# A four-layer graph network on one Trainium2 core: variances of a layer's late part by ACT, sends held back, ring places freed by the block

## The chip, the cores and the metric

The kernel runs on one core of a Trainium2 chip, in one launch. The engines are TensorE (PE; its weight loads are listed as PEld), VectorE (DVE), ScalarE (ACT), GpSimd (POOL) and SyncE (SP). The metric is the device time of the launch in microseconds (us). The kernel before takes 1677.57 us, the median of eight runs, which lie between 1672.64 and 1680.2.

## The reference

4096 nodes with 256 features each go through four graph attention layers over the same symmetric 0/1 adjacency matrix with about nine neighbours a row, the node itself included. Each layer adds to x what attention makes of a normed x:

```python
h = jnp.maximum(_layernorm(x, axis=-1), 0.0)        # (x - mean) / sqrt(var + 1e-5), then relu
x = x + layer(h, adj, ...)

# layer 0, 4 heads of 64
Wh = (h @ W).reshape(n, heads, d)
e = leaky_relu(s_i[:, None, :] + s_j[None, :, :], 0.2)   # s: Wh times the halves of a
e = where(adj == 0, -inf, e); alpha = softmax(e, axis=1)
out = elu(einsum('ijh,jhd->ihd', alpha, Wh))

# layer 1, one head:  h @ W + softmax(masked leaky_relu(s1 + s2, 0.01)) @ node
# layer 2, four heads: like layer 0 with biases, slope 0.2, no elu
# layer 3, four heads: softmax(q k^T / 8 + mask) v, with q, k, v = h @ Wq + bq, ...
```

The adjacency matrix is an input, so the kernel has to find the neighbours itself.

## The kernel before, in words

The rows are sorted by their number of neighbours and cut into 32 blocks of 128 rows. All rows of a block have the same number of slots (`CAPS[b]`, 23 in block 0 down to 3 in block 31), of which layers 1 to 3 gather at most 15; rows of block 0 with more neighbours share an extra place. A *gather* (`fetch`, L993) is an indirect DMA issued by POOL: 128 rows of a table in DRAM, one for each partition, go to one place of a ring in SBUF (`RING` = 18432 floats a partition; 69 places of 264 floats in the late part of layer 0 and in layer 2, 64 of 288 in layer 1, 36 of 512 in layer 3). A *send* (`send`, L1010) is the opposite: 128 rows go to their places in a table or, in layer 3, in the output. The tables `tab[0]` to `tab[3]` hold what the neighbours of each layer need.

The stages, by the profile:

- 0 to some 362 us: the matrix is read, the neighbour lists are made, the rows are sorted, and the first six slots of layer 0 are worked off on the way.
- `late()`, 364.7 to 542.7: the rest of layer 0, in 19 groups (`LATE`) of one or two blocks, 14 of which still have something to gather (17 places for block 0 in turn 3, then 8, 7 and fewer a block down to 1). It is pipelined by hand: turn i does `scores(i)`, then parts of `settle` for groups i-2, i-1, i-3 and i-2, then `weigh(i)`, then a part of `settle(i-1)`. PE, DVE, ACT and SP run in the order in which the program is written. POOL's order is chained by `turn` dependences: `fill(i)` first sends every finished block (`deliver`), and then issues the gathers of the groups up to i+4.
- `layer(1)` 542.7 to 903.3, `layer(2)` to 1268.2, `layer(3)` to the end: blocks in the order `ORDER`, gathers ahead as far as the ring has room (`fill`), every engine in program order.

In a turn of `late()`, `scores` adds the two halves of the score (L1132), takes the leaky relu (L1136), has ACT copy the row's old maximum beside them (L1137), takes the maximum (L1140), subtracts it (L1141) and has ACT take exp (L1146). `weigh` makes the sum and the shares (L1162 to L1166), multiplies the row's earlier result and the gathered rows with them (L1170, L1184) and sums them on PE (L1178, L1190). `settle` has five parts:

1. ACT makes exp of the sum, minus 1 (L1201, L1202);
2. DVE makes elu plus x (L1204, L1205), and `norms_of` the mean and variance, `bn_stats` and `bn_aggr` a block (L642, L643); ACT then makes 1/sqrt(var + eps) to first order by Ln, Identity, Exp and Square (L648, L652, L653, L655);
3. DVE does a Newton step (L659, L661, L664), ACT norm and relu (L1214), PE the transposes (L1221);
4. ACT copies them (L1224), PE multiplies with layer 1's weights (L986);
5. DVE adds layer 1's own product to x (L1231), ACT writes scores and list beside it (L1232, L1233), and the block is ready to send to `tab[1]`.

`known()` makes what later stages need of the lists (as float numbers, with marks where a slot is empty); it is called in turn 1. It waits on DVE for the lists' reload (L804) and has one iota on POOL (L807).

In `layer(l)`, `weigh` sums in one PSUM tile: x (L1450), the row's own share (made at L1454, product at L1458), then the gathered slots, multiplied by DVE eight at a time (L1466) and two to a matmul (L1471). A gather that reuses a place of the ring waits for all the products that read it, as the tile framework finds them. `settle` sums the two halves of the PSUM tile; in layer 3 that is the result, one of three buffers of two kinds in turn (L1487), which is appended to `made`. After each block `third` sends what is in `made`:

```python
while made and (len(made) > 1 or todo == []):
    self.send(*made.pop(0))
```

so one result is held back as long as there are gathers left (`todo`), and then all go.

Of the kernel before, what the change touches and what calls it, by code (L numbers as in the profile page):

```python
# [19 lines left out]
P = 128  # L20
# [60 lines left out]
class Sparse:  # L81
# [938 lines left out]
    def layers(self):  # L1020
        tc, nc, nt = self.tc, self.nc, self.nt
        with ExitStack() as ctx:
            big = self.big = ctx.enter_context(tc.tile_pool(name="s_big", bufs=1))
            self.pacc = ctx.enter_context(tc.tile_pool(name="s_pacc", bufs=4, space=PSUM))
            shares = ctx.enter_context(tc.tile_pool(name="s_pe", bufs=1, space=PSUM))
            self.pp = ctx.enter_context(tc.tile_pool(name="s_pp", bufs=3, space=PSUM))

            self.turns = 0
            self.shares = shares.tile([P, IB], F32, name="s_shares")

            rx = self.all = big.tile([P, nt, D + WL], F32, name="s_rx")
# [9 lines left out]
            self.has = big.tile([P, nt, CAPS[0]], F32, name="s_has")  # L1041
            E = mybir.EngineType
# [13 lines left out]
    def late(self):  # L1056
# [26 lines left out]
            self.fetched = f  # L1083
            return f

        def deliver():
            while pending:
                b = pending.pop(0)
                s = self.send(self.tab[1], self.own(b), self.listed[b]).ins
                if self.fetched is not None:  # L1090
                    self.turn(s, self.fetched)
                between.append(s)
                self.tc.declare_no_dep(s, group="rows", reason="places differ")
                self.tc.add_to_no_dep_group("rows", s)
                self.told.append(s)

        def fill(i):
            nonlocal at
            deliver()
            while todo and todo[0] <= i + 4:  # L1100
                m, K = size(todo[0])
                s = (at if at + m * K <= slots else 0) if K else 0
                if any(s < e and b < s + m * K for b, e in held.values()):
                    return
                j = todo.pop(0)
                for u, b in enumerate(LATE[j]):
# [88 lines left out]
        def settle(i):  # L1195
# [9 lines left out]
            nc.vector.scalar_tensor_tensor(xt, acc, 0.0, ex, ALU.max, ALU.add)  # L1205
            norm = self.norms_of(pool, xt if m > 1 else xt[:, 0, :], m, f"0_{i}", self.minus)
            for _ in range(m if m > 1 else 0):
                next(norm)
            next(norm)
            yield  # L1210
            rn = next(norm)
            h = part(i, D, 2 * D)
            for u in range(m):
                nc.scalar.activation(  # L1214
                    h[:, u, :], xt[:, u, :], AF.Relu,
                    bias=rn[:, m + u : m + u + 1], scale=rn[:, u : u + 1],
                )
            pt = self.pp.tile([P, IB], F32, tag="ps", name=f"s_pht_0_{i}")
            for u in range(m):
# [24 lines left out]

        for i in range(len(LATE) + 3):
            fill(i)
            if i == 1:
                self.known()
            if i == 5:
                self.share_place()  # L1250
            if i < len(LATE):
                scores(i)
            go_on(i - 2)
            go_on(i - 1)
            go_on(i - 3)
            go_on(i - 2)
            if i < len(LATE):
                weigh(i)
                del held[i]
            go_on(i - 1)  # L1260
        deliver()

    def layer(self, l):
# [5 lines left out]
        ring = self.ring[:, : slots * wide].rearrange("p (k w) -> p k w", w=wide)  # L1269
        todo, held, at = list(ORDER), {}, 0  # L1270
        made = []

        def fill(i):
            nonlocal at
            while todo and nt - len(todo) <= i + AHEAD:
# [11 lines left out]
                if l == 3:  # L1287
                    vs[j] = self.pool.tile([P, D], F32, name=f"s_vself_{j}", tag="vself", bufs=5)
                    nc.sync.dma_start(out=vs[j], in_=self.tab[3][ts(j, P), D:])
                for k in range(K):  # L1290
                    at_k = self.near[:, j, k : k + 1]
                    g = self.fetch(ring[:, s + k, :], self.tab[l], at_k).ins
                    for told in self.told:
                        self.tc.add_manual_dep(
                            g, told.name,
# [32 lines left out]
        def third(d):  # L1328
            if d in rows:
                next(rows.pop(d), None)  # L1330
            while made and (len(made) > 1 or todo == []):
                self.send(*made.pop(0))

        S, N = 1, 2
        for i in range(nt):
# [10 lines left out]
            del held[b]  # L1346
            settle(c)
        z, y, x, w = ORDER[-1:-5:-1]

# [9 lines left out]
    def scores(self, l, b, mine, g):  # L1359
# [8 lines left out]
        if l < 3:  # L1368
# [2 lines left out]
                nc.scalar.activation(e[:, :G, 0], g[:, :G, D], AF.Identity, bias=src)  # L1371
                nc.scalar.activation(e[:, K, :], mine[:, D : D + H], AF.Identity, bias=src)
            else:
                nc.vector.tensor_tensor(e[:, K, :], mine[:, D : D + H], src, ALU.add)
# [11 lines left out]
            nc.vector.scalar_tensor_tensor(ek, ek, slope, ek, ALU.mult, ALU.max)  # L1386
        else:
            q = self.shares[:, IB - D :]
            nc.scalar.copy(q, mine[:, 0:D])
# [31 lines left out]
    def mutual(self, b, g):  # L1421
# [7 lines left out]
        nc.vector.tensor_reduce(self.has[:, b, :K], eq[:, :K, :], AX.X, ALU.max)  # L1429

    def weigh(self, l, b, me, g, made):

# [7 lines left out]
        if tot is None:  # L1440
# [9 lines left out]
        nc.tensor.matmul(  # L1450
            acc[:, 1, :], lhsT=self.ident, rhs=self.x[b], start=True, stop=False
        )
        mev = pool.tile([P, D], F32, name=f"s_me_{l}_{b}", tag="me", bufs=3)
        nc.vector.tensor_tensor(  # L1454
            mev.rearrange("p (h d) -> p h d", h=H), me.rearrange("p (h d) -> p h d", h=H),
            p[:, K, :].unsqueeze(2).to_broadcast([P, H, D // H]), ALU.mult,
        )
        nc.tensor.matmul(acc[:, 0, :], lhsT=self.ident, rhs=mev, start=False, stop=False)  # L1458
        if more:
            rows = self.more_rows(l, p, g[:, KEPT, :])  # L1460
            nc.tensor.matmul(acc[:, 0, :], lhsT=self.to_row, rhs=rows, start=False, stop=False)
        step = 2 if b in ORDER[-2:] else AT_ONCE
        for k0 in range(0, G, step):
            m = min(step, G - k0)
# [1 line left out]
            nc.vector.tensor_tensor(  # L1466
                v, v, p[:, k0 : k0 + m, :].unsqueeze(3).to_broadcast([P, m, H, D // H]), ALU.mult
            )
            for k in range(k0, k0 + m, 2):
                n = min(2, G - k)  # L1470
                nc.tensor.matmul(  # L1471
                    acc[:, 0:n, :], lhsT=self.ident, rhs=g[:, k : k + n, v0 : v0 + D],
                    start=False, stop=(k + 2 >= G),
                )
        return acc

    def settle(self, l, b, acc, made):
# [5 lines left out]
        if l == 3:  # L1483
# [4 lines left out]
            made.append((self.out, self.own(b), y))  # L1488
            yield None
            return  # L1490
        nc.vector.tensor_reduce(xt, acc.rearrange("p u d -> p d u"), AX.X, ALU.add)
        yield from self.normed(pool, xt, f"{l + 1}_{b}")

    def advance(self, l, b, ht, made):
# [35 lines left out]
    def symmetric(self):  # L1530

        nc, ok = self.nc, self.ok[:, 4:5]
        nc.vector.scalar_tensor_tensor(
            self.has, self.away[:, :, : CAPS[0]], 1.0 / FAR, self.has, ALU.mult, ALU.max
        )
        nc.vector.tensor_reduce(self.both[:, 0:1], self.has, AX.XY, ALU.min)
        nc.vector.tensor_reduce(ok, self.both, AX.X, ALU.min)
        nc.vector.tensor_scalar(ok, ok, 0.5, None, ALU.is_ge)
# [564 lines left out]
```

## Time and profile before

| what | value |
|---|---|
| median of 8 runs | 1677.57 us (1672.64 to 1680.2) |
| the profiled execution: its time, its span | 1676.78 us, 1675.1 us |
| mean clock granted to TensorE | 0.817 of full speed |
| busy: PE, DVE, ACT, POOL | 1099.8, 1104.6, 541.5, 1143.8 us |
| gathers from the ring stages on (L993 into `s_ring`) | 900, 952 ns each |
| sends of layer 0's late part, of layer 3 | 32, 32 |

In a line of the profile the first number (or the first two) is a start or a busy time in us; `x900` is a number of instructions; `out<-in` names the tiles; a bracket or a last column tells how long the engine had been idle before, and what ended that. "issue" stands for idle time in which the engine waited for nothing that the profile shows. All times are of one execution.

### The profile page before, as it was taken

The numbers are of one execution on the slowest core, as the hardware profiler recorded it, in microseconds if no ns is written. First come the engines' busy times: TensorE is split into PE (matmuls) and PEld (weight loads), VectorE is DVE, ScalarE is ACT, GpSimd is POOL, SyncE is SP. The second block draws the span as 40 slices with busy tenths as digits, with TensorE's granted clock in tenths as the row PEclk, the third lists the DMA queues.
The fourth block names the chain that finished last, engine by engine and source line by source line (L and its number), as shares of the span: only waits on it lengthen the run. The fifth ranks groups of instructions, "written<-read, shape, count | busy, mean of one in ns | idle before, by whom it ended". The sixth has DMA issues, their size and how long they took to land. (4 is left out here: it accounts for less than half of the span.)

```text
span 1675.1 us, 14506 instructions
## 1 busy us (share of the span) xinstructions
PE 1099.8 (66%) x3035; PEld 572.7 (34%) x3035; DVE 1104.6 (66%) x2651; ACT 541.5 (32%) x1754; POOL 1143.8 (68%) x1241
## 2 busy tenths in 40 slices
PE   5868878705775377777773787878782655556445
PEld 4523333203443144444442344444441322222222
DVE  5669899816885255555552576667674897877776
ACT  6966664003344133333332133333341000000000
POOL 1277777767774777777773777777755777777774
PEclk9969999857898678788786798989996777677777
DMA  7899999466552444444442444444435776767663
GB/s 267 301 395 394 353 394 326 145 218 166 153 167 69 119 128 133 131 132 130 133 131 65 116 132 133 134 132 133 133 109 169 222 212 196 210 191 212 196 188 112
DMA packets 125912, 309.11 MB, mean 185 GB/s; under 512 B 35028, under 2 KB 53463, under 8 KB 125816
## 3 DMA queue, kind: packets, MB, share of 16 engines
q0 software_dynamic: 66832, 203.64, 41.7%
q1 hardware_dynamic: 58984, 104.46, 17.5%
q8 instruction: 28, 0.46, 0.1%
q14 instruction: 68, 0.56, 0.1%
HBM read 273.00 MB, written 35.00 MB: 184 GB/s over the span
## 5 line engine op out<-in xcount | busy, mean ns | idle before, releaser
L993 POOL DMA_INDIRECT s_ring<-s_tab,s_near x900 | 857.0, 952 | 325.9 <-issue 240.5
L1471 PE MATMUL s_acc<-s_ring,s_ident 128*128 128x512 f32 (+1 forms) x858 | 425.9, 647 | 28.9 <-DVE s_ring L1466 28.9
L993 POOL DMA_INDIRECT s_g<-s_tab,s_keep x192 | 182.8, 952 | 130.9 <-DMA s_raw<-in_adj_dram 66.5
L1471 PEld LDWEIGHTS s_acc<-s_ring,s_ident 128*128 128x128 f32 x858 | 185.0, 220 | 249.9 <-issue 181.8
L1466 DVE TENSOR_TENSOR s_ring<-s_ring,s_shares 128x2048 f32<-128x2048 f32 (+1 forms) x153 | 232.8, 1552 | 0.0
L1458 PE MATMUL s_acc<-s_me,s_ident 128*128 128x256 f32 x192 | 77.6, 494 | 130.8 <-DVE s_me L1454 130.8
L277 ACT ACTIVATE s_low<-s_raw 128x1024 fp8e4<-128x1024 int32 x128 | 135.1, 1055 | 65.7 <-DMA s_raw<-in_adj_dram 64.5
L986 PE MATMUL s_ps<-s_we_l,s_ht 128*128 128x264 f32 x256 | 95.8, 520 | 91.8 <-ACT s_ht L976 68.2
L1418 ACT ACTIVATE s_shares<-s_e 128x40 f32<-128x40 f32 (+7 forms) x64 | 13.0, 203 | 344.4 <-DVE s_e L1415 344.3
L986 PE MATMUL s_ps_kv<-s_wkv,s_ht 128*128 128x512 f32 x128 | 80.4, 761 | 63.6 <-ACT s_ht L976 63.6
L1394 DVE TENSOR_TENSOR s_ring<-s_ring,s_shares 128x2048 f32<-128x2048 f32 (+7 forms) x47 | 78.7, 1675 | 65.3 <-DMA s_ring<-s_tab,s_near 45.4
L519 PE MATMUL s_pt<-s_low,s_mark_True 128*128 128x512 fp8e4 x256 | 83.3, 405 | 54.4 <-DVE s_cand L531 48.7
L531 DVE MAX8 s_cand<-s_pt 128x8 f32<-128x256 f32 x256 | 93.1, 416 | 13.8 <-PE s_pt L529 13.8
L1426 DVE TENSOR_SCALAR s_eq<-s_ring,s_own_f 128x207 bf16<-128x207 f32 (+12 forms) x32 | 12.2, 382 | 136.0 <-DMA s_ring<-s_tab,s_near 135.7
L986 PEld LDWEIGHTS s_ps<-s_we_l,s_ht 128*128 128x128 f32 x256 | 57.5, 243 | 118.8 <-ACT s_ht L976 80.7
L629 PE MATMUL s_ae<-s_g,s_ident 128*128 128x512 f32 x192 | 93.9, 619 | 3.5 <-DVE s_g L620 3.5
L956 ACT ACTIVATE s_y<-s_mv,s_eps 128x1 f32<-128x1 f32 x64 | 18.9, 295 | 232.3 <-DVE s_mv L953 125.7
L1458 PEld LDWEIGHTS s_acc<-s_me,s_ident 128*128 128x128 f32 x192 | 43.0, 240 | 148.8 <-DVE s_me L1454 142.9
L1397 DVE TENSOR_REDUCE s_e<-s_ring 128x32 f32<-128x2048 f32 (+7 forms) x47 | 78.9, 1679 | 1.6
L1375 DVE TENSOR_TENSOR s_e<-s_ring,s_rx 128x36 f32<-128x36 f32 (+12 forms) x32 | 6.3, 197 | 103.6 <-DMA s_ring<-s_tab,s_near 81.2
L1450 PE MATMUL s_acc<-s_rx,s_ident 128*128 128x256 f32 x192 | 67.6, 439 | 0.0
L519 PEld LDWEIGHTS <-s_mark_True 128*128 128x128 bf16 x256 | 23.2, 101 | 107.7 <-issue 63.6
(284 smaller groups left out, 1787.6 us busy)
## 6 DMA issues: line engine op xcount, KB each, us to landing
s_raw<-in_adj_dram SPq DMA_DIRECT2D x128, 512.0 KB, 9.7
s_ring<-s_tab,s_near POOLq DMA_INDIRECT x900, 2.9
s_rx<-s_placed SPq DMA_DIRECT2D x32, 262.0 KB, 3.1
s_tab<-s_kv SPq DMA_DIRECT2D x32, 256.0 KB, 2.5
s_tab<-s_rx SPq DMA_DIRECT2D x32, 132.0 KB, 2.0
s_keep<-in_x_dram SPq DMA_DIRECT2D x8, 512.0 KB, 8.9
s_vself<-s_tab SPq DMA_DIRECT2D x32, 128.0 KB, 3.4
s_tab<-s_keep SPq DMA_DIRECT2D x7, 528.0 KB, 3.9
```

The lines of the kernel that those rows point to most:

```text
L277: nc.scalar.activation(low[r][:, quarter(q)], raw.pop(q), AF.Copy, saturate=False, accum_out=self.sums[:, r, h : h + 1],)
L519: nc.tensor.matmul(pt, lhsT=self.mark[k], rhs=lo[:, k * PAIR + g * IB : k * PAIR + (g + 1) * IB], start=(k == 0), stop=False,)
L531: nc.vector.max(out=cand[:, g * (IB // CH) + k, :], in_=pt[:, ts(k, CH)])
L629: nc.tensor.matmul(acc, lhsT=self.ident, rhs=g[:, :, k, 0:D], start=False, stop=(k == E - 1))
L986: self.nc.tensor.matmul(ps[:, :width], lhsT=ht[:, c, :], rhs=w[:, c, :], start=(c == 0 and bias is None), stop=(c == KC - 1),)
L993: return self.nc.gpsimd.indirect_dma_start(out=out, out_offset=None, in_=table[:, :], in_offset=bass.IndirectOffsetOnAxis(ap=idx, axis=0),)
L1394: nc.vector.tensor_tensor(kq, kq, q.unsqueeze(1).to_broadcast([P, m, D]), ALU.mult)
L1397: nc.vector.tensor_reduce(e[:, k0 : k0 + m, :], kq.rearrange("p k (h d) -> p k h d", h=4), AX.X, ALU.add)
L1450: nc.tensor.matmul(acc[:, 1, :], lhsT=self.ident, rhs=self.x[b], start=True, stop=False)
L1458: nc.tensor.matmul(acc[:, 0, :], lhsT=self.ident, rhs=mev, start=False, stop=False)
L1466: nc.vector.tensor_tensor(v, v, p[:, k0 : k0 + m, :].unsqueeze(3).to_broadcast([P, m, H, D // H]), ALU.mult)
L1471: nc.tensor.matmul(acc[:, 0:n, :], lhsT=self.ident, rhs=g[:, k : k + n, v0 : v0 + D], start=False, stop=(k + 2 >= G),)
```

## The change

Five things change.

- In `settle` of the late part, L1205 becomes one instruction for each block, which also writes the row's sum. The bn instructions are gone: ACT makes the negative mean of the sum (Copy), then for each block a Square with the mean as bias whose sum is the variance times 256, and then the same Ln, Identity, Exp and Square.
- `deliver` in `fill` holds up to eight finished blocks back; layer 3's `third` holds up to three results back instead of one.
- `known()` is called in turn 3 instead of turn 1.
- In layers 1 to 3 the row's own product is now the last matmul of a block, and the first slot has a matmul of its own. The first gather into a place of the ring that a block held waits for that last matmul alone; waits for the block's other products are declared needless.
- A few more dependences that a later instruction implies are declared needless.

```diff
-        def deliver():
-            while pending:
+        def deliver(held_back=0):
+            while len(pending) > held_back:
...
-            deliver()
+            deliver(8)
...
-            nc.vector.scalar_tensor_tensor(xt, acc, 0.0, ex, ALU.max, ALU.add)
-            norm = self.norms_of(pool, xt if m > 1 else xt[:, 0, :], m, f"0_{i}", self.minus)
-            for _ in range(m if m > 1 else 0):
-                next(norm)
-            next(norm)
+            y = pool.tile([P, 8, 2], F32, name=f"s_y_0_{i}", tag="y0", bufs=3)
+            sum_, minus, q, log, root, less, r, at = (y[:, k, 0:m] for k in range(8))
+            for u in range(m):
+                nc.vector.scalar_tensor_tensor(
+                    xt[:, u, :], acc[:, u, :], 0.0, ex[:, u, :], ALU.max, ALU.add,
+                    accum_out=sum_[:, u : u + 1],
+                )
+            act = nc.scalar.activation
+            act(minus, sum_, AF.Copy, scale=-1.0 / D)
+            junk = pool.tile([P, D], F32, name=f"s_junk_{i}", tag="junk", bufs=1)
+            for u in range(m):
+                act(
+                    junk, xt[:, u, :], AF.Square, bias=minus[:, u : u + 1],
+                    accum_out=q[:, u : u + 1],
+                )
+            act(log, q, AF.Ln, bias=self.eps, scale=1.0 / D)
+            act(less, q, AF.Identity, bias=self.minus, scale=-0.5 / D)
+            act(root, log, AF.Exp, scale=-0.5)
+            act(log, root, AF.Square)
             yield
-            rn = next(norm)
+            nc.vector.tensor_tensor(less, log, less, ALU.mult)
+            nc.vector.scalar_tensor_tensor(r, less, 1.5, root, ALU.add, ALU.mult)
+            nc.vector.tensor_tensor(at, minus, r, ALU.mult)
...
-            if i == 1:
+            if i == 3:
                 self.known()
...
+                ends = [
+                    e for a, b, e in past if a < (s + room) * wide and s * wide < b
+                ]
...
                     g = self.fetch(ring[:, s + k, :], self.tab[l], at_k).ins
+                    if k == 0:
+                        for _, last in ends:
+                            self.tc.add_manual_dep(
+                                g, last.name,
...
+                    for some, _ in ends:
+                        for m in some:
+                            self.tc.declare_no_dep(g, m, reason="its block's last is waited for")
...
-            while made and (len(made) > 1 or todo == []):
+            while made and (len(made) > 3 or todo == []):
                 self.send(*made.pop(0))
...
-        nc.tensor.matmul(acc[:, 0, :], lhsT=self.ident, rhs=mev, start=False, stop=False)
...
-            for k in range(k0, k0 + m, 2):
-                n = min(2, G - k)
...
+            while k < k0 + m:
+                n = min(2, k0 + m - k) if some else 1
...
+        last = nc.tensor.matmul(
+            acc[:, 0, :], lhsT=self.ident, rhs=mev, start=False, stop=True
+        ).ins
+        self.tc.declare_no_dep(last, own.ins, reason="the slots' products come after it")
+        self.read = (some, last)
```

More of the change, by code (lines that the diff above doesn't have):

```diff
@@ L1041, in layers @@
             self.has = big.tile([P, nt, CAPS[0]], F32, name="s_has")
+            self.past, self.took_x, self.seen = [], {}, []
             E = mybir.EngineType
@@ L1215, in settle @@
                     h[:, u, :], xt[:, u, :], AF.Relu,
-                    bias=rn[:, m + u : m + u + 1], scale=rn[:, u : u + 1],
+                    bias=at[:, u : u + 1], scale=r[:, u : u + 1],
                 )
@@ L1271, in layer @@
         made = []
+        past = self.past
         def fill(i):
@@ L1289, in fill @@
                     nc.sync.dma_start(out=vs[j], in_=self.tab[3][ts(j, P), D:])
+                ends = [
+                    e for a, b, e in past if a < (s + room) * wide and s * wide < b
+                ]
+                past[:] = [
+                    (a, b, e) for a, b, e in past if not (a < (s + room) * wide and s * wide < b)
+                ]
                 for k in range(K):
@@ L1292, in fill @@
                     g = self.fetch(ring[:, s + k, :], self.tab[l], at_k).ins
+                    if k == 0:
+                        for _, last in ends:
+                            self.tc.add_manual_dep(
+                                g, last.name,
+                                mybir.DependencyInfo(
+                                    mybir.DependencyClass.Sync, mybir.DependencyReason.DATA
+                                ),
+                                reason="the block's slots are free",
+                            )
+                    for some, _ in ends:
+                        for m in some:
+                            self.tc.declare_no_dep(g, m, reason="its block's last is waited for")
                     for told in self.told:
@@ L1345, in layer @@
             sums[b] = self.weigh(l, b, vs.pop(b) if l == 3 else self.rows[b][:, 0:D], g, p)
-            del held[b]
+            start, end = held.pop(b)
+            past.append((start * wide, end * wide, self.read))
             settle(c)
@@ L1373, in scores @@
             else:
-                nc.vector.tensor_tensor(e[:, K, :], mine[:, D : D + H], src, ALU.add)
+                first = nc.vector.tensor_tensor(e[:, K, :], mine[:, D : D + H], src, ALU.add)
                 nc.vector.tensor_tensor(
@@ L1385, in scores @@
             slope = 0.01 if l == 1 else 0.2
-            nc.vector.scalar_tensor_tensor(ek, ek, slope, ek, ALU.mult, ALU.max)
+            steep = nc.vector.scalar_tensor_tensor(ek, ek, slope, ek, ALU.mult, ALU.max)
+            if l == 2:
+                self.tc.declare_no_dep(steep.ins, first.ins, reason="another sum comes after it")
         else:
@@ L1428, in mutual @@
         )
-        nc.vector.tensor_reduce(self.has[:, b, :K], eq[:, :K, :], AX.X, ALU.max)
+        self.seen.append(
+            nc.vector.tensor_reduce(self.has[:, b, :K], eq[:, :K, :], AX.X, ALU.max).ins
+        )
     def weigh(self, l, b, me, g, made):
@@ L1449, in weigh @@
         acc = self.pacc.tile([P, 2, D], F32, tag="acc", name=f"s_acc_{l}_{b}")
-        nc.tensor.matmul(
+        self.took_x[b] = nc.tensor.matmul(
             acc[:, 1, :], lhsT=self.ident, rhs=self.x[b], start=True, stop=False
         )
+        some = []
         mev = pool.tile([P, D], F32, name=f"s_me_{l}_{b}", tag="me", bufs=3)
-        nc.vector.tensor_tensor(
+        own = nc.vector.tensor_tensor(
             mev.rearrange("p (h d) -> p h d", h=H), me.rearrange("p (h d) -> p h d", h=H),
@@ L1457, in weigh @@
         )
-        nc.tensor.matmul(acc[:, 0, :], lhsT=self.ident, rhs=mev, start=False, stop=False)
         if more:
             rows = self.more_rows(l, p, g[:, KEPT, :])
-            nc.tensor.matmul(acc[:, 0, :], lhsT=self.to_row, rhs=rows, start=False, stop=False)
+            some.append(
+                nc.tensor.matmul(
+                    acc[:, 0, :], lhsT=self.to_row, rhs=rows, start=False, stop=False
+                ).ins
+            )
         step = 2 if b in ORDER[-2:] else AT_ONCE
@@ L1468, in weigh @@
             )
-            for k in range(k0, k0 + m, 2):
-                n = min(2, G - k)
-                nc.tensor.matmul(
-                    acc[:, 0:n, :], lhsT=self.ident, rhs=g[:, k : k + n, v0 : v0 + D],
-                    start=False, stop=(k + 2 >= G),
-                )
+            k = k0
+            while k < k0 + m:
+                n = min(2, k0 + m - k) if some else 1
+                some.append(
+                    nc.tensor.matmul(
+                        acc[:, 0:n, :], lhsT=self.ident, rhs=g[:, k : k + n, v0 : v0 + D],
+                        start=False, stop=False,
+                    ).ins
+                )
+                k += n
+        last = nc.tensor.matmul(
+            acc[:, 0, :], lhsT=self.ident, rhs=mev, start=False, stop=True
+        ).ins
+        self.tc.declare_no_dep(last, own.ins, reason="the slots' products come after it")
+        self.read = (some, last)
         return acc
@@ L1490, in settle @@
             return
-        nc.vector.tensor_reduce(xt, acc.rearrange("p u d -> p d u"), AX.X, ALU.add)
+        s = nc.vector.tensor_reduce(xt, acc.rearrange("p u d -> p d u"), AX.X, ALU.add)
+        self.tc.declare_no_dep(
+            s.ins, self.took_x.pop(b).ins, reason="the sum's last product comes after it"
+        )
         yield from self.normed(pool, xt, f"{l + 1}_{b}")
@@ L1532, in symmetric @@
         nc, ok = self.nc, self.ok[:, 4:5]
-        nc.vector.scalar_tensor_tensor(
+        all_of = nc.vector.scalar_tensor_tensor(
             self.has, self.away[:, :, : CAPS[0]], 1.0 / FAR, self.has, ALU.mult, ALU.max
         )
+        for i in self.seen[:-1]:
+            self.tc.declare_no_dep(all_of.ins, i, reason="the last of them is waited for")
         nc.vector.tensor_reduce(self.both[:, 0:1], self.has, AX.XY, ALU.min)
```

## The prediction

> **What bounds the kernel now.** I read the page first, for the engines' shares; then the table by stage; then POOL's and DVE's timelines, since no share is near 100%.
>
> ```profile
> PE 1099.8 (66%) x3035; PEld 572.7 (34%) x3035; DVE 1104.6 (66%) x2651; ACT 541.5 (32%) x1754; POOL 1143.8 (68%) x1241
> L993 POOL DMA_INDIRECT s_ring<-s_tab,s_near x900 | 857.0, 952 | 325.9 <-issue 240.5
> ```
>
> The busiest engine, POOL, does little but issue row gathers, and its idle time before them is put down mostly to "issue", to no wait. The stages (columns: length; busy time and count of PE, PEld, DVE, ACT, POOL; clock, DMA share, GB/s) are the late part of layer 0 and layers 1, 2 and 3:
>
> ```profile
> 364.70:542.70 178.00, 111.11 (x360) 70.50 (x360) 123.20 (x389) 69.11 (x245) 123.95 (x125) 0.82 0.52 148
> 542.70:903.30 360.60, 253.52 (x674) 142.12 (x674) 172.92 (x383) 124.60 (x512) 255.18 (x270) 0.80 0.45 123
> 903.30:1268.20 364.90, 271.02 (x742) 146.93 (x742) 233.16 (x574) 123.45 (x483) 256.99 (x270) 0.87 0.45 125
> 1268.20:1675.10 406.90, 214.94 (x423) 96.70 (x423) 305.71 (x414) 22.29 (x95) 288.11 (x302) 0.73 0.65 194
> ```
>
> POOL's timeline inside layer 1 shows what "issue" is:
>
> ```profile
> 691.41 0.95 POOL L993 DMA_INDIRECT s_ring<-s_tab,s_near  x1 [0.30 <-issue]
> 692.66 0.95 POOL L993 DMA_INDIRECT s_ring<-s_tab,s_near  x1 [0.30 <-issue]
> ```
>
> One gather starts every 1.25 us. 270 of them are 338 of layer 1's 360.6 us, and the rest is the change of layers (the longest gap before an L993 is 23.5 us for "issue" and 26.0 us for "s_tab<-s_kv"). So layers 1 and 2 are as long as POOL's queue. Layer 3 has 270 gathers and 32 sends of the output (L1010). Its end is not compute, which does its last sum at 1665.21, but the sends behind the last gather:
>
> ```profile
> 1648.41 0.94 POOL L993 DMA_INDIRECT s_ring<-s_tab,s_near  x1 [0.30 <-issue]
> 1649.66 1.00 POOL L1010 DMA_INDIRECT out_dram<-s_out,s_near  x1 [0.30 <-DVE s_ring L1394]
> 1653.39 0.99 POOL L1010 DMA_INDIRECT out_dram<-s_out,s_near  x1 [2.73 <-DVE s_e L1415]
> 1656.59 0.97 POOL L1010 DMA_INDIRECT out_dram<-s_out,s_near  x1 [2.22 <-DVE s_ring L1466]
> ...
> 1670.77 0.97 POOL L1010 DMA_INDIRECT out_dram<-s_out,s_near  x1 [2.50 <-issue]
> ```
>
> A send next to a gather takes 1.3 us of the queue; next to a send 3.2 to 4.4 us, because the program lets each send wait for the one before, till it has landed (median 2.7 us from issue). These seven start 21.1 us apart in all, a mean of 3.52.
>
> In the late part POOL is ahead: it idles 17.7 us in all before its last sends, and DVE is 123 of 178 us busy. DVE goes through its program in order, and once in each group waits for ACT:
>
> ```profile
> 515.47 0.69 DVE L1205 SCALAR_TENSOR_TENSOR s_rx<-s_acc,s_ex 128x512 f32<-128x512 f32 x1
> 516.19 0.43 DVE L642 BATCH_NORM_STATS2 s_st<-s_rx 128x6 f32<-128x256 f32 x1
> 517.18 0.18 DVE L643 BATCH_NORM_AGGREGATE s_mv<-s_st 128x2 f32<-128x6 f32 x1
> 518.33 0.17 DVE L1140 TENSOR_REDUCE s_m<-s_e 128x8 f32<-128x16 f32 x1 [0.60 <-ACT s_e L1137]
> ```
>
> ```profile
> 517.40 0.30 ACT L648 ACTIVATE s_y<-s_mv,s_eps 128x2 f32<-128x2 f32 x1 [2.17 <-DVE s_mv L643]
> 518.12 0.18 ACT L1137 COPY s_e<-s_rx 128x8 f32<-128x8 f32 x1
> ```
>
> L1205 makes the row, four bn instructions its mean and variance, ACT (L648 to L655) the root, and only behind these in ACT's queue stands the copy L1137 which DVE's next maximum, L1140, needs. That chain, L1205 to L1140, is 2.86 us in a group of two blocks and 2.06 to 2.15 in a group of one (501.67 to 503.73, 479.72 to 481.87).
>
> **Variances by ACT.** Removed from DVE are 32 x (0.414 + 0.182) = 19.1 us of bn. But a group of two is now: two sums of 128x256 (a pair of that shape on DVE, L1231, takes 0.75), hand-over to ACT 0.04, the mean's Copy 0.22 (L653 to L655 is that far apart), two Squares with a bias each, their two reads, then the old 0.90 (517.40 to 518.30) and 0.03. For Square and read:
>
> ```profile
> L1526 ACT ACTIVATION_READ_ACCUMULATOR s_sq<-s_rx 128x1 f32 x32 | 6.0, 186 | 0.0
> L1214 ACT ACTIVATE s_rx<-s_rx,s_rn 128x256 f32<-128x256 f32 x32 | 17.8, 594 | 5.8 <-DVE s_rn L664 5.8
> ```
>
> Square without a bias tile takes 0.41 (L1526's own row); L1214, with bias and scale tiles, 0.594, two in 1.09. I take 0.50, between them. Sum: 0.75 + 0.04 + 0.22 + 1.00 + 0.37 + 0.93 = 3.31, against 2.86: +0.45 (0.27 to 0.55 by the two rows). A group of one: 0.42 + 0.04 + 0.22 + 0.50 + 0.19 + 0.93 = 2.30, +0.15 to +0.24. The work leaves a busy engine and comes back as a longer wait, since one block after the other goes through ACT. Queued behind the wait on DVE are L1140, the norm's L659 to L664, the x sum and the whole weighing; PE and ACT wait for those. From the 17-gather group's turn (391 us) on there are 11 groups of two and 6 of one; where a turn has no scores, DVE's L659 waits for the same chain (0.88 at 525.57): 11 x 0.45 + 6 x 0.15 = 5.9. In about six of them DVE later waits for something else anyway (four for gathers, 4.2 us; two for PE's L986, 3.3 us), where the delay is absorbed: minus 2. No row shows a DVE sum written out beside the result. Below: nothing. Above: ACT's read, 0.19, in each of 28 blocks, 5.2. I take 0.09, the distance from one small DVE operation to the next (the L643 at 472.79 to the L642 at 472.88): +2.5. Late part: +6.4; ends +1 and +11.
>
> The Trainium skill, "VectorE: DVE Perf Modes", section "Two Vector instructions with no wait between them", says that an operation which also writes its accumulator is two instructions; it gives no time. With ACT's time for the second the late part would be +9.
>
> **Sends held back, late part.** Up to eight finished blocks stay unsent while gathers go first; in the order of the changed program 22 sends, not 14, follow the last gather. The last gathers come some 8 x 1.3 = 10 us sooner, but DVE did not wait for them there. Sends there need not wait for each other (1.3 us apart at 509.77 to 513.61), and POOL's 17.7 us idle takes eight more. The last pair still follows the last group. Zero; were the idle time gone, 10 us.
>
> **Lists needed later.** The call known() moves two groups on. Its 6.67 us DVE wait (376.74) goes, but the scores of the 17-gather group wait till 390.86 (3.23 us idle) whatever stands in front. Its iota on POOL still stands in front of all gathers, so no queue loses by it. Zero; its 1.9 us of DVE work, if that cover is gone.
>
> **Layers 1 and 2, and the ring.** Releasing a ring place by its block's last product drops most of POOL's waits. The gap between gathers is 0.305 us with none and with one or two waiting instructions ahead, so nothing is gained. Refills come 40 to 69 us after the products; nothing is lost. In layer 3 the first three have only 5.7 us, of which the product moved to the block's end takes about 2: zero again, 4 us once if that is gone. That product adds no columns; 72 more matmuls, PE idle a quarter of the time: zero, at most one 128x256 matmul (L1458's 0.49) at each of three ends. The dropped dependences move nothing on a bound queue.
>
> **Sends held back, layer 3.** Up to three results wait instead of one. Four neighbouring pairs are left in mid-layer, as before (stalls of 2.62 to 3.13 us), but nine sends, not seven, follow the last gather. It ends 2 x 1.31 = 2.6 us sooner; then eight distances instead of six: 8 x 3.17 (shortest) to 8 x 3.52 (mean) is 25.4 to 28.2, minus 21.1, minus 2.6: +1.7 to +4.5. I take 3.1. A result's buffer also waits longer for its send, some 1.7 us for DVE, which is 75% busy there and catches up: zero, 1.7 at most.
>
> The Trainium skill, "DMA: Bandwidth & Descriptors", section "Anatomy of one DMA — SWDGE (gpsimd) path", puts most of a DMA's fixed 2.0 us on the confirmation that the data has landed, which speaks against lining up sends that wait for one another. By its 2.0 behind 0.97 of issue, estimated, eight distances are 23.8 us and the tail about 0; the trace's 2.7 decides.
>
> **Sum.** 6.4 + 3.1 = +9.5 on the profiled run: 1676.78 (span 1675.1 and 1.7 around it) becomes 1686.3. The median of the eight runs is 0.8 higher, so 1687.
>
> **The rivals.** *DVE's relief counts (faster).* If ACT's chain lies beside DVE work, DVE gives back per group of two 1.17 of bn less 0.06 for the split sum, per group of one 0.6: 11 x 1.11 + 6 x 0.6 = 15.8, less 2.5 for the sums written out: 13 us, with the tail 1667. It decides where L1140 no longer waits; against it, 11 waits of 4.8 us there already. *It cancels (same).* The four mid-layer stalls go because held sends find the one before landed, 11.5 us, against 9.5: 1675.6; or late slack absorbs all and the tail is shortest: 1679. Against the first: the pairs are still neighbours. *Slower still.* Accumulator reads at 0.19 (+2.7), the longest Square and the buffers' 1.7: 1692. *The change does not do what it says:* if the sends' order came out as before, +6.4 alone, 1684.
>
> **How the numbers follow.** This kernel's measurement can tell about 0.2%, 3.4 us, from no change. Forecast 0.55, slower still 0.10, cancelled 0.14, relief 0.21. The low end takes in the cases where about half of the relief reaches the end, and cuts the rest off; the high end adds the unknown sums' bounds to the slower case.
>
> **Signs.** Right: no bn in the late part, L1140's idle up from 4.8 to some 10 us, layer 1's first gather near 549 instead of 542.7; layers 1 and 2 unchanged within 1 us; nine last sends 3.2 to 3.5 us apart. Wrong: that first gather before 542, L1140 without idle, fewer mid-layer stalls, or a gather in layer 3 waiting for PE.

## The result and the profile after

The changed kernel takes 1685.19 us (median of 14 runs, 1682.83 to 1689.57); the kernel before, in 38 runs, 1676.99. The ratio is 1.005, with a 95% interval from 1.004 to 1.006: slower by 8.2 us, where 1687 and +9.5 were forecast. The profiled execution took 1684.62 us, span 1682.7.

The engines' shares on the page hide where that comes from. DVE and PE are less busy than before, ACT 24 us more, POOL the same:

```profile
PE 1081.4 (64%) x3179; PEld 600.1 (36%) x3179; DVE 1086.5 (65%) x2632; ACT 565.2 (34%) x1837; POOL 1141.9 (68%) x1241
L993 POOL DMA_INDIRECT s_ring<-s_tab,s_near x900 | 855.7, 951 | 327.6 <-issue 289.1
```

The table by stage does show it (columns as before; stages again cut at POOL's first gather of each):

```profile
364.38:546.85 182.47, 111.97 (x360) 71.08 (x360) 105.33 (x370) 92.30 (x328) 122.69 (x126) 0.81 0.50 144
546.85:907.55 360.70, 253.50 (x722) 150.23 (x722) 173.39 (x383) 124.32 (x512) 255.29 (x270) 0.80 0.44 123
907.55:1272.61 365.06, 271.78 (x790) 156.08 (x790) 233.08 (x574) 123.42 (x483) 257.04 (x270) 0.87 0.45 125
1272.61:1682.70 410.09, 196.00 (x471) 105.32 (x471) 305.17 (x414) 22.27 (x95) 287.40 (x302) 0.73 0.65 193
```

The late part is 4.5 us longer although DVE is busy for 105.3 us there instead of 123.2. Layers 1 and 2 are as long as they were, to 0.2 us. From layer 3's first gather to its last send there were 402.5 us (1268.24 to 1670.77) and are now 405.6 (1272.61 to 1678.22): 3.1 more. The parts account for nearly all of it: 4.1 us at layer 1's first gather, 0.25 in layers 1 and 2 and 3.1 up to the last send are 7.45 of the 7.6 us by which the span grew.

DVE's timeline in the late part shows what took the place of the bn instructions. It is a group of two, as in the lines of before:

```profile
510.87 0.42 DVE L1209 SCALAR_TENSOR_TENSOR s_rx<-s_acc,s_ex 128x256 f32<-128x256 f32 x1
511.22 0.08 DVE L1209 DVE_READ_ACCUMULATOR s_rx<-s_acc,s_ex 128x1 f32 x1
511.22 0.42 DVE L1209 SCALAR_TENSOR_TENSOR s_rx<-s_acc,s_ex 128x256 f32<-128x256 f32 x1
511.56 0.08 DVE L1209 DVE_READ_ACCUMULATOR s_rx<-s_acc,s_ex 128x1 f32 x1
511.56 0.16 DVE L1133 TENSOR_TENSOR s_e<-s_ring,s_rx 128x8 f32<-128x8 f32 x1
511.76 0.17 DVE L1137 SCALAR_TENSOR_TENSOR s_e<-s_e 128x8 f32<-128x8 f32 x1
514.11 0.17 DVE L1141 TENSOR_REDUCE s_m<-s_e 128x8 f32<-128x16 f32 x1 [2.19 <-ACT s_e L1138]
```

DVE is through by 511.9 and then stands for 2.19 us, till ACT's copy L1138 is done. ACT's timeline has what stands in front of that copy: two Squares and their reads.

```profile
511.68 0.20 ACT L1214 ACTIVATE s_y<-s_y 128x2 f32<-128x2 f32 x1 [2.54 <-DVE s_rx L1209]
511.92 0.51 ACT L1217 ACTIVATE s_junk<-s_rx,s_y 128x256 f32<-128x256 f32 x1
512.33 0.19 ACT L1217 ACTIVATION_READ_ACCUMULATOR s_junk<-s_rx,s_y 128x1 f32 x1
512.55 0.51 ACT L1217 ACTIVATE s_junk<-s_rx,s_y 128x256 f32<-128x256 f32 x1
512.97 0.19 ACT L1217 ACTIVATION_READ_ACCUMULATOR s_junk<-s_rx,s_y 128x1 f32 x1
513.18 0.29 ACT L1221 ACTIVATE s_y<-s_y,s_eps 128x2 f32<-128x2 f32 x1
513.90 0.18 ACT L1138 COPY s_e<-s_rx 128x8 f32<-128x8 f32 x1
```

From the first L1209 to the maximum L1141 it is 3.24 us, where it was 2.86. In the list of DVE's waits from 391 us to the end of the late part (us in total, times, longest) the line of that wait has grown; the first line is the kernel before, the second the changed one:

```profile
DVE s_m L1140 <- ACT s_e L1137: 4.8, 11, 0.6
DVE s_m L1141 <- ACT s_e L1138: 22.9, 12, 2.2
```

At the end of layer 3 POOL's timeline has nine sends behind the last gather:

```profile
1649.39 0.95 POOL L993 DMA_INDIRECT s_ring<-s_tab,s_near  x1 [0.30 <-issue]
1650.64 0.99 POOL L1010 DMA_INDIRECT out_dram<-s_out,s_near  x1 [0.30 <-issue]
1653.76 0.99 POOL L1010 DMA_INDIRECT out_dram<-s_out,s_near  x1 [2.13 <-DMA out_dram<-s_out,s_near]
1657.48 0.97 POOL L1010 DMA_INDIRECT out_dram<-s_out,s_near  x1 [2.74 <-DVE s_ring L1511]
...
1678.22 0.97 POOL L1010 DMA_INDIRECT out_dram<-s_out,s_near  x1 [2.21 <-DMA out_dram<-s_out,s_near]
```

Where the bracket names out_dram, the wait is named as what it is, a send's landing. Where it names a DVE line, it was a landing too: the send at 1653.76 landed 2.93 us after its start, and the next one started 0.79 us later, as in the rest of the row (0.75 to 0.79 us after the landing; 0.27 once). DVE's last sum ends at 1666.28, 11.9 us before the last send starts (5.6 us in the kernel before).

### The profile page after: what moved, and what is told of

It reads as the page before. It is cut to its first block, busy times and chain, and to the rows that moved or that the text cites. A ratio compares the mean times of both kernels' runs of the same rounds, so it can differ in the third digit from the quotient of the medians.

```text
span 1682.7 us, 14690 instructions
## 1 busy us (share of the span) xinstructions
PE 1081.4 (64%) x3179; PEld 600.1 (36%) x3179; DVE 1086.5 (65%) x2632; ACT 565.2 (34%) x1837; POOL 1141.9 (68%) x1241
## 5 line engine op out<-in xcount | busy, mean ns | idle before, releaser
L1518 PEld LDWEIGHTS s_acc<-s_ring,s_ident 128*128 128x128 f32 x1002 | 215.2, 220 | 361.8 <-DVE s_ring L1511 194.9
L993 POOL DMA_INDIRECT s_g<-s_tab,s_keep x192 | 182.7, 951 | 130.7 <-DMA s_raw<-in_adj_dram 66.2
L986 PE MATMUL s_ps<-s_we_l,s_ht 128*128 128x264 f32 x256 | 99.6, 537 | 91.9 <-ACT s_ht L976 68.7
L986 PE MATMUL s_ps_kv<-s_wkv,s_ht 128*128 128x512 f32 x128 | 81.5, 771 | 62.6 <-ACT s_ht L976 62.6
L986 PEld LDWEIGHTS s_ps<-s_we_l,s_ht 128*128 128x128 f32 x256 | 59.9, 253 | 119.9 <-ACT s_ht L976 81.2
L1433 DVE TENSOR_TENSOR s_ring<-s_ring,s_shares 128x2048 f32<-128x2048 f32 (+7 forms) x47 | 78.5, 1671 | 28.4 <-DMA s_ring<-s_tab,s_near 20.4
L986 PEld LDWEIGHTS s_ps_kv<-s_wkv,s_ht 128*128 128x128 f32 x128 | 26.3, 227 | 90.8 <-ACT s_ht L976 70.2
L1238 PE MATMUL s_pht<-s_ident,s_rx 128*128 128x128 f32 x64 | 14.2, 329 | 68.0 <-DMA s_ring<-s_tab,s_near 41.8
```

The lines of the kernel that those rows point to most:

```text
L986: self.nc.tensor.matmul(ps[:, :width], lhsT=ht[:, c, :], rhs=w[:, c, :], start=(c == 0 and bias is None), stop=(c == KC - 1),)
L993: return self.nc.gpsimd.indirect_dma_start(out=out, out_offset=None, in_=table[:, :], in_offset=bass.IndirectOffsetOnAxis(ap=idx, axis=0),)
L1433: nc.vector.tensor_tensor(kq, kq, q.unsqueeze(1).to_broadcast([P, m, D]), ALU.mult)
L1518: nc.tensor.matmul(acc[:, 0:n, :], lhsT=self.ident, rhs=g[:, k : k + n, v0 : v0 + D], start=False, stop=False,).ins
```

## The experiments

The two theories: the loss is the longer chain of ACT in the late part plus the longer row of sends in layer 3 (mine); or it comes from another part of the change (the sends held back in the late part, the lists, the ring). Since the parts act in different stages, one kernel can carry several of them, and each is read in its own stage. "Late part" is from the first gather at its start to layer 1's first gather; "layer 3" from its first gather to its last send.

In ten of the twelve runs (e1 to f4, g2 and g3) TensorE seemed to pause: its results came 10 to some 70 us late at a time (the last section shows one such place). The kernel before beside them was as slow and took 2044 to 2047 us there. Of these runs mainly the ratios and what the pauses don't touch are used; where a stage's length is compared, it is between such runs, with one profile each.

### Variances by ACT and held results, alone (g1, f1, e1, e2)

The edits, put into the kernel before: the whole of the change's first part, and the line in `third`. The first alone is e1, the second alone e2, both together f1 and g1:

```diff
-            norm = self.norms_of(pool, xt if m > 1 else xt[:, 0, :], m, f"0_{i}", self.minus)
...
+            act(minus, sum_, AF.Copy, scale=-1.0 / D)
...
-            while made and (len(made) > 1 or todo == []):
+            while made and (len(made) > 3 or todo == []):
```

> The kernel before with the variances by ACT and up to three results held back in layer 3, nothing else, taken again because TensorE paused for 10 to 70 us at a time in the runs before. Theory: late part 3.5 to 4.7 us longer than 178.0; in layer 3 the last gather 3 to 5 us sooner after the first than 380.2, nine last sends 3.1 to 4.6 us apart, the last send 0.5 to 3 us later against the layer's start than 402.5; the time 4 to 7 us above the kernel before. Rival (the late part's held sends and lists, or the ring, cost it): late part within 1 us of 178.0, layer 3 within 0.5 us of 402.5.

Measured: 1684.32 us against 1676.87, ratio 1.004 (1.0027 to 1.0052). The late part is 182.7 us long, 4.7 more than before and 0.2 more than with the whole change. Its wait on DVE is that of the whole change:

```profile
DVE s_m L1140 <- ACT s_e L1137: 22.9, 12, 2.2
```

In layer 3 the last gather starts 376.9 us after the first (380.2 before), nine sends 3.1 to 4.6 us apart follow, and the layer is 405.8 us long, 3.3 more than before. So these two edits make the whole loss, and the other parts of the change, taken together, are worth nothing that shows: late part 182.5 with them, layer 3 405.6. The rival falls. Neither edit was run alone without pauses; that each makes its own stage's loss rests on their acting in different stages.

> The kernel before with the variances by ACT alone. Theory (ACT's chain in front of the copy that the maximum waits for grows by some 0.4 us a group): layer 1's first gather 3.5 to 4.5 us later than the 542.7 of before, the late part's whole loss; the rest as before: time +4, 1681. Rival (the sends held back or the lists' new place make the late part longer): the first gather within 1 us of before, time 1677.

> The kernel before with up to three results held back in layer 3 instead of one, nothing else. Theory (nine last sends, not seven, each waiting for the one before, start 3.45 us apart): the last gather some 3 to 5 us earlier than 1648.4, the last send 2 to 4 us later than 1670.8; time +1 to +3, 1679. Rival (what layer 3 lost is the ring's release): last send within 1 us of before, time 1677.

> The kernel before with the variances by ACT in the late part and up to three results held back in layer 3, the other parts as before. The two act in different stages, so the stages are read apart. Theory: late part 3.5 to 4.5 us longer than 178.0, DVE's wait before the maximum some 2.2 us a group of two; layer 3's last gather some 4 us sooner than 380.2 after its first, nine last sends 3.1 to 4.6 us apart, the last 2 to 3 us later against the layer's start. Time 1677 + 6. Rival (the held sends of the late part or the ring cost it): late part within 1 us of 178.0, layer 3 within 1 us of 402.5, time 1677.

Ratios 0.9994 (0.997 to 1.0018), 0.9997 (0.9973 to 1.0022) and 1.0013 (0.9984 to 1.0042). The time says nothing here: where PE pauses, 4 us on DVE or at the end are lost in its pauses. The stages point the same way as in g1, but weakly: late parts of 224.9 and 226.3 us with the variances, 221.2 and 223.2 without (e2, e4).

### The other half (e3, e4, f2)

```diff
-            deliver()
+            deliver(8)
...
-            if i == 1:
+            if i == 3:
                 self.known()
```

is e3; e4 is the ring's release, the sums' order and the dropped dependences as in the change; f2 has both.

> The kernel before with up to eight finished blocks held back in the late part and the lists' marks made two groups later, nothing else. Theory (both lie under the in-order chain of DVE and ACT): the last gather of the late part some 10 us earlier, layer 1's first gather within 0.7 us of 542.7, time within 1 us of before. Rival (the gathers that come sooner feed DVE sooner): the first gather 2 us or more earlier, time 1675 or less.

> The kernel before with the ring's release by a block's last product, that product moved to the end, the first slot by itself, and the needless dependences dropped; variances, sends and lists as before. Theory: layers 1 and 2 within 0.3 us of 360.6 and 364.9; in layer 3 two gathers wait for PE's last product, 1.6 and 0.7 us, which shifts the layer's end by 1 to 2.5 us; time +1 to +2.5, 1679. Rival (dropped waits give POOL time): layers 1 and 2 shorter by over 2 us each, time 1673.

> The other half of the change: eight finished blocks held back and the lists' marks two groups later in the late part, the ring's release by the block's last product in layers 1 to 3; variances and layer 3's sends as before. Theory: late part within 0.7 us of 178.0 though its last gather comes some 10 us sooner; layers 1 and 2 within 0.3 us of 360.6 and 364.9; in layer 3 two refills wait for PE, 1 to 2.5 us in all, and the end moves by as much. Time 1677 + 0 to 3. Rival (gathers sooner and fewer waits give time back): late part under 176, or layers 1 and 2 shorter by over 1 us, time 1674 or less.

Ratios 1.0144 (1.0104 to 1.0185), 0.9821 (0.9786 to 0.9855) and 1.0017 (0.999 to 1.0043). None of this answers what was asked, as PE paused; it showed something else. The late part of e3 and f2 was 253.5 and 253.7 us, some 30 more than in e1, e2, e4 and f1. Layer 2 was 463.0 us in e4 and 474.0 in f2, against 497 to 503 in e1, e2, e3 and f1 (of the four runs below, 474.4 and 481.8 with that part, 497.7 and 488.1 without). So when PE falls behind, holding back sends and lists costs, and the ring's release and the new order of the sums pay. Which piece of either does so was not taken apart. That both are worth nothing when PE keeps up rests on the difference between the whole change and g1.

### Chain covered, sends free (h1; f3, f4, g2, g3)

Would the bn instructions' time come back if DVE had work during ACT's chain? And are the landings between sends the tail? Two edits, in the kernel before (f3, g2) and in the changed one (f4, g3, h1). In the late part `ahead` issues ACT's copy of the old maximum, which is taken out of `scores`, and the order of the parts of `settle` is another (`go_on(k)` runs the next part for group k). In layer 3 a send no longer waits for the one before it, and a small memset on POOL stands before each:

```diff
-            go_on(i - 2)
-            go_on(i - 1)
             go_on(i - 3)
-            go_on(i - 2)
+            go_on(i - 1)
             if i < len(LATE):
                 weigh(i)
                 del held[i]
+            if i + 1 < len(LATE):
+                ahead(i + 1)
+            go_on(i - 2)
             go_on(i - 1)
+            go_on(i - 2)
...
-                self.send(*made.pop(0))
+                nc.gpsimd.memset(self.gap, 0.0)
+                s = self.send(*made.pop(0)).ins
+                self.tc.declare_no_dep(s, group="results", reason="places differ")
+                self.tc.add_to_no_dep_group("results", s)
```

> The changed kernel with ACT's chain of the late part covered (the copy of the old maximum a turn ahead, the norm's second part behind the weighing) and with sends of layer 3 that don't wait for each other, once more. Theory: no wait of DVE before the maximum; late part shorter than the 178.0 of the kernel before, 162 to 172; layer 3's sends 1.3 to 1.6 us apart where results are ready, the four stalls in the middle gone, its last send some 390 us after its start instead of 405.6; time 20 to 30 us below the kernel before. Rival (late part bound by PE's sums; layer 3's tail by compute): late part 177 or more, layer 3 over 400.

Measured: 1718.55 us against 1679.44, ratio 1.0242 (1.0228 to 1.0256). The expectation was right in layer 3 and wrong in the late part. POOL's timeline of h1 at the end:

```profile
1699.67 0.95 POOL L993 DMA_INDIRECT s_ring<-s_tab,s_near  x1 [0.30 <-issue]
1700.61 0.11 POOL L1382 MEMSET s_gap<- 128x1 f32 x1
1700.92 0.99 POOL L1010 DMA_INDIRECT out_dram<-s_out,s_near  x1 [0.19 <-issue]
1702.21 0.99 POOL L1010 DMA_INDIRECT out_dram<-s_out,s_near  x1 [0.19 <-issue]
...
1714.99 0.96 POOL L1010 DMA_INDIRECT out_dram<-s_out,s_near  x1 [4.38 <-DVE s_out L1558]
1716.84 0.97 POOL L1010 DMA_INDIRECT out_dram<-s_out,s_near  x1 [0.77 <-DVE s_out L1558]
```

Sends are now 1.29 us apart, the four stalls in mid-layer are gone, and the last three wait for their results (L1558; the first of them for 1.11 us), no longer for a landing. Layer 3 is 386.1 us long instead of 405.6, 19.5 less: the landings between sends are shown to be the tail, and a good deal of the middle.

In the late part DVE no longer waits before the maximum, but the part takes 236.7 us, 54 more. The longest in total of DVE's waits there:

```profile
DVE s_rx L1260 <- PE s_ps L986: 89.5, 28, 8.5
```

My order put the x sum (L1260) right behind the product that it needs, and that product (L986) on PE behind the sums of the turn. ACT's copy of the transposes (L1253), which the product needs, still stands behind ACT's chain. The wait was not covered but moved to a longer one. How much of the 54 us comes from that order alone was not taken apart: the granted clock was 0.73 in this stage instead of 0.81, and PE was busy for 138.3 us instead of 112.0. So whether the relief of DVE would count under a real cover stays open.

> The kernel before (variances by DVE's bn) with two edits. Late part: ACT's copy of the old maximum is issued a turn ahead of the norm's chain, and the norm's second part moves behind the weighing, so that ACT's chain lies beside DVE's products. Layer 3: the output's sends no longer wait for each other; a small memset on POOL stands before each. Theory (DVE waits for the chain; the tail is the sends' landings): late part 170 to 174 instead of 178.0; layer 3's sends 1.5 us apart, its four stalls in the middle gone, layer 3 some 390 instead of 402.5; time 1677 - 18. Rival (late part bound by PE's sums and the copy of them, and the tail by compute): late part 177 or more, layer 3 over 400.

> The changed kernel with the same two edits: chain of ACT beside DVE's weighing, free sends. Theory (with the chain covered, the bn instructions taken off DVE count at last): late part shorter than that of the kernel before with the same cover, by 4 to 13 us, so 160 to 168; layer 3 some 390; time 1677 - 25. Rival (DVE's time is not what binds even then): late part within 2 us of the other one.

> The kernel before (variances by DVE's bn) with two edits, taken again because TensorE paused in the first run. Late part: ACT's copy of the old maximum a turn ahead of the norm's chain, and the norm's second part behind the weighing, so that ACT's chain lies beside DVE's products. Layer 3: the output's sends no longer wait for each other; a small memset on POOL before each. Theory: late part 170 to 175 instead of 178.0, no wait of DVE before the maximum; layer 3's sends 1.3 to 1.6 us apart where results are ready, no stalls of 2.6 us in the middle, layer 3's last send some 390 instead of 402.5 after its start; time 15 to 20 us below the kernel before. Rival (late part bound by PE's sums and their copies; tail by compute): late part 177 or more, layer 3 over 400.

> The changed kernel with the same two edits, taken again for the same reason. Theory (with ACT's chain covered, the 19 us of bn taken off DVE count): late part shorter than that of the kernel before with the same cover by 4 to 13 us; layer 3 as there within 1.5 us, though up to three results are held back, since sends that don't wait cost 1.3 us each wherever they stand; time 20 to 30 us below the kernel before. Rival (DVE's time doesn't bind even then, or ACT's does): late part within 2 us of the other one or longer.

Ratios 1.0177 (1.0132 to 1.0223), 1.024 (1.0194 to 1.0286), 1.0248 (1.0209 to 1.0287) and 1.0239 (1.0192 to 1.0286), with PE pausing. Late parts of 267 to 307 us fit the same wrong order, but pauses are in them too. What the pauses don't touch agrees with h1: sends whose results are ready start 1.27 to 1.31 us apart in all four.

Free sends with everything else as in the kernel before were not run. Taken from h1's layer 3, where up to three results are held back and the ring is the changed one, an estimate is 1677 - (402.5 - 386.1) = 1661 us, below both kernels.

## Why the prediction was right, and where its steps were not

**Late part: forecast +6.4, measured +4.1** at layer 1's first gather (542.72 to 546.85), 4.5 in length. The mechanism is the one forecast, a chain put in front of the copy that DVE waits for, and its size too: 3.24 us for a group of two (3.31 forecast), 2.26 for a group of one (2.30). A Square took 0.51 us (0.50 taken), from one to the next 0.63 (0.69 taken). The mis-sized term is the sums written out by DVE, +2.5. The trace now has a row for them: DVE_READ_ACCUMULATOR, 0.08 us, and it costs nothing that shows, as the next instruction starts with it (511.22 both). The two halves and their reads take 0.69 us to the next instruction's start (510.87 to 511.56); the one 128x512 instruction of before took 0.72 (515.47 to 516.19). Without that term the sum is +3.9. That this lies so near the 4.1 is in part luck: over the 17 groups the chain grew by 5.1 us (5.9 forecast), and 1.0 of that did not reach layer 1 (2 forecast). DVE's short waits before the scores, 1.9 us behind those of the 17-gather group, fell to 0.2, but its waits for PE's L986 stayed (3.3 and 3.4). The rule of the Trainium skill ("VectorE: DVE Perf Modes", section "Two Vector instructions with no wait between them") holds: it is two instructions. ACT's 0.19 was the wrong price for the second.

**The signs.** DVE's wait before the maximum was to grow from 4.8 to some 10 us; it grew to 22.9. The step counted only what the chain grew by. But the bn instructions had been DVE's part of that chain, and when they left, their time became wait as well: DVE is 17.9 us less busy in the late part, its wait before the maximum 18.1 longer. (In turns without scores its wait before the Newton step grew as well, from 3.5 to 8.9 us in all.) One of the signs named for a wrong forecast came: gathers in layer 3 waited for PE. The mid-layer stalls were not fewer (still four), but shorter. Both are below; neither decided the time.

**Late sends and lists: zero, measured zero.** The last gather of the late part came 12 us sooner (494.88 instead of 507.08; 10 forecast) and nothing followed from it: layer 1's first gather is at 546.85 with the held sends and 546.79 without (g1). DVE's wait before the scores of the 17-gather group ends at 390.73 (390.86 before), as forecast, and is 9.5 us long instead of 3.2.

**Layers 1 and 2: zero, measured +0.1 each.** POOL's gap stayed 0.30 us with fewer waits.

**Ring: zero, with up to 4 us.** Two refills of layer 3 did wait for the block's last product, 1.60 us at 1316.43 and 0.72 at 1339.32. So the step that found 5.7 us of room enough for a product of about 2 was wrong for these two; the 2.3 us lie within the 4 that the bound allowed. Nothing of it reaches the end: with it layer 3 is 405.6 long, without it (g1) 405.8. The stalls of the mid-layer sends are 9.6 us in all with it and 10.9 without; why they differ was not looked into.

**Layer 3's sends: forecast +3.1, measured +3.1**, the size by its own terms only in part. Forecast were a last gather 2.6 us sooner and a row 5.7 longer. Measured are 3.4 sooner (376.8 us after the first instead of 380.2; the mid-layer stalls fell from 11.5 to 9.6) and a row from last gather to last send 6.5 longer (28.8 instead of 22.4), eight distances of 3.45 us on average (3.12 to 4.62, where 3.2 to 3.5 were named). Two misses of 0.8 us cancel; that the sum came out to within 0.1 us is luck. The estimate with the fixed 2.0 us that the Trainium skill gives ("DMA: Bandwidth & Descriptors", section "Anatomy of one DMA — SWDGE (gpsimd) path") was 2.97 us a distance and a tail of 0, too little. It was not the landing that it had too short: in this row the sends landed 2.4 to 3.9 us after their start, 2.7 on average. It left out that the next send starts only some 0.7 us after the landing. DVE's wait for a result's buffer was larger than the 1.7 us named, 34.8 us in all, and cost nothing that shows, as its wait for gathers shrank (45.4 to 20.4) and its last sum came no later against the layer's start.

**The rivals.** DVE's relief did not count: the maximum still waits, 22.9 us in all instead of 4.8. Cancelling did not happen: the pairs of sends stayed and so did most of their stalls.

## What to carry to other kernels

Before work is moved off a busy engine, find the instruction of that engine that next waits for the engine it is moved to: if the moved work lies in front of what is waited for, the relief comes back as wait, and more (here 17.9 us less work of DVE, 18.1 us more wait before the maximum alone). Holding transfers back helps only if they may overlap at the end. Where each waits for the landing of the one before, every transfer moved behind the last gather costs its issue and its landing (here 3.45 us each, against 1.29 without the wait), and the thing to remove first is the wait between them.

## What the runs showed that was not expected

In ten runs, results of TensorE came long after the end of the matmuls in the records. In e1's timeline, where transposes (L974) are recorded as done at 766.7, their reader on ACT waited until 791.6, and so did the next product:

```profile
791.63 0.37 ACT L976 COPY s_ht<-s_pht 128x256 f32<-128x256 f32 x1 [24.32 <-remote]
792.05 1.25 PE L986 MATMUL s_ps<-s_we_l,s_ht 128*128 128x264 f32 x2 [24.74 <-issue]
```

"remote" means that no instruction was found that ended the wait; by its semaphore it was PE's. The granted clock was 0.91 in the 25 us before this place and 0.57 in the 25 us of the pause, and 0.752 on average over the run, against 0.817. Every kernel of those runs, the one before too, took about 2000 to 2110 us, and the parts of this change weighed differently there than in the runs that the forecast was for. The ten runs were on two chips (numbers 5 and 11), g1 and h1 on two others (13 and 3). Whether that is the reason, and why TensorE paused, was not found.
